# Masks of listed blocks moved into the rows of the feature tables (four graph-attention layers, one core)

## The chip, the cores and the metric

The kernel runs on one core of one Trainium2 chip. The metric is the device time of one execution in microseconds (us). TensorE (PE) multiplies matrices; its weight loads are shown as PEld. VectorE (DVE), ScalarE (ACT) and GpSimd (POOL) work on elements, SyncE (SP) issues DMAs. Indirect DMAs, which gather rows by a list of indices, are issued by GpSimd.

## The reference

Four layers of graph attention act on 4,096 nodes with 256 features, all with the same 4096 x 4096 adjacency. Each layer normalizes its input, applies a ReLU, and adds the attention's output to its input:

```
h = relu(layernorm(x))
layer 0: x += softmax(mask(leaky(s_i + t_j))) @ (h @ W.T + b)
layer 1: x += elu(softmax(mask(leaky(s_i + t_j))) @ (h @ W))
layer 2: four heads of 64 columns, each with its own s, t and W; no elu
layer 3: two softmaxes, of e and of -e; the two averages of h, the second negated,
         side by side, times wtrans, then elu
s, t = projections of the transformed rows (s by target node, t by source node)
```

Adjacency is random with a falling density: node i and node j are connected with a probability proportional to 1/sqrt((1+i)(1+j)), so early nodes have many sources and late ones few.

## The kernel before, in words

**Tiles.** Nodes stand in 32 tiles of 128 (NT). Targets are grouped in 8 blocks of 4 tiles (IT). Sources are grouped in chunks of 4 tiles (CH). The first chunk of sources (DP tiles) is always used in full ("pre").

**Dense and listed targets.** For a dense block, every source tile is used: one step weighs 128 sources for 512 targets on VectorE and multiplies them on TensorE (four matmuls of 128x257). For a listed target tile T, the used sources are collected in a list with room for CAPS[T] x 128 of them (6 to 12 for T from 4 on), and each step gathers 128 feature rows with an indirect DMA, weighs them and multiplies them once. DENSE = (4, 2, 1, 1) says how many blocks are dense in each layer; the others are listed. So layers 0 to 3 have 105, 174, 218 and 218 feature gathers.

**Where the operands come from.** Each layer's projected rows, with two more columns for the weights, are written to a DRAM table (`table[l]`, `node_rows`, lines 706 and 708) and gathered from there into `s_gg` (line 1189; pools of 7 buffers in layer 0, `gat0`, and 9 later, `gat`). In layer 0 the adjacency is read once: `mask_chunk` turns a loaded chunk into bytes on VectorE (line 1277) and writes it to `mask_t[b]`, one DRAM table for each block (line 1279). Dense blocks of layer 0 use the chunk at once; those of layers 1 to 3 load it back (`s_ms`, line 1390, beside the features `s_gs`, line 1388). For listed tiles, `gather_masks` (line 895) gathers the 128-byte mask rows of the same sources, once for each (T, k), into `mlist`, which stays on chip for all layers: 218 gathers in all.

**Lists.** In layer 0, blocks 4 to 7 are read as "side" chunks between the dense steps (`sides`). When all chunks of a block have been seen, `list_sources` builds its four lists, piece by piece.

**Order.** `run` walks a plan of steps written out by hand. Each step is fetched (gathers and loads are issued), begun, weighed and multiplied at fixed distances, LEAD = (0, 2, 3, 6), so that a step is multiplied six plan steps after its fetch. After each step, some pieces of other work are done: `posts` (projections for the next layer, ends of tiles), `lists_q` (list building) and `gather_masks`, in numbers given by `rates`. In layer 0, listed steps start beside the dense ones at plan step LISTED0 and are taken one or two at a time; layer 1 has 16 dense steps alone, then puts two dense steps behind each of its 24 listed tiles (16 to 31, then 8 to 15). In layers 2 and 3, tiles 8 to 31 come first and tiles 4 to 7 last. GpSimd's queue holds its instructions in just the order in which they are written; those of the other engines are ordered by a scheduler. A listed tile first makes sure that all masks of that tile are gathered.

**The end of a kernel.** A flag says whether a list was too short; then a dense version would run instead. It doesn't run with these inputs.

Of the kernel before, what the change touches and what calls it, by code (L numbers as in the profile page):

```python
# [8 lines left out]
F32 = mybir.dt.float32  # L9
F16 = mybir.dt.float16  # L10
U8 = mybir.dt.uint8
# [6 lines left out]
P = 128  # L18
N = 4096
D = 256  # L20
# [432 lines left out]

DP = CH
# [5 lines left out]
LISTED0 = 40  # L460
# [7 lines left out]
GW = tuple(h * p for h, p in zip(LH, PART))  # L468
LEAD = (0, 2, 3, 6)
# [3 lines left out]
def list_layers(ctx: ExitStack, tc: tile.TileContext, a: dict, out: bass.AP, flag):  # L473
# [38 lines left out]
    mask_t = [dram.tile([N + 1, IB], U8, name=f"mask_t{b}", tag=f"mask_t{b}") for b in range(NIB)]  # L512
    table = [dram.tile([N + 1, GW[l]], F32, name=f"table{l}", tag=f"table{l}") for l in range(4)]

    def table_rows(t, jt):

        r0 = jt // CH * CH * P
        r0 += 1 if r0 >= HALF else 0
        return t[r0 : r0 + CH * P, :].rearrange("(p k) d -> p k d", k=CH)

# [5 lines left out]
    def weights(l, pool, prep, q):  # L526
# [11 lines left out]
        L.table = table[l]  # L538
# [123 lines left out]
    def node_rows(L, T0):  # L662
# [29 lines left out]
        for k, T in enumerate(tiles):  # L692
# [3 lines left out]
            hT = rows.tile([P, 2, P], F32, name=f"s_hT_{u}_{k}", tag="hT")  # L696
# [4 lines left out]
        for k, T in enumerate(tiles):  # L701
# [3 lines left out]
            if L.l == 0 and T % CH == CH - 1:  # L705
                nc.sync.dma_start(table_rows(L.table, T), L.g[:, T - CH + 1 : T + 1, :])
            elif L.l > 0:
                nc.sync.dma_start(table_rows(L.table, T)[:, T % CH, :], g)
# [89 lines left out]
    def list_sources(ib, seen, pool, consts):  # L798
# [82 lines left out]

    masks_of = [
        (T, k)
        for b0, b1 in ((DENSE[0], NIB), (DENSE[1], DENSE[0]), (1, DENSE[1]))
        for T in range(b0 * IT, b1 * IT)
        for k in range(CAPS[T])
    ]

    def gather_masks(n, tile=None):

        for T, k in list(masks_of):
            if not n or tile is None and T not in index:
                break
            if tile in (None, T):
                nc.gpsimd.indirect_dma_start(  # L895
                    out=mlist[:, OFFS[T] + k, :],
                    out_offset=None,
                    in_=mask_t[T // IT],
                    in_offset=bass.IndirectOffsetOnAxis(ap=index[T][:, k : k + 1], axis=0),
                    element_offset=T % IT * P,  # L900
                )
                masks_of.remove((T, k))
                n -= 1

# [42 lines left out]
    class Unit:  # L947
# [4 lines left out]
        def __init__(u, L, T0, nt, n, get, big=None, heads=None, like=None, cost=1.7, nact=0, rates=(2, 0, 0), per=1):  # L952
# [205 lines left out]
    def run(plan):  # L1158

        n = len(plan)  # L1160
        for p in range(n + LEAD[3]):
# [5 lines left out]
            if p >= LEAD[3]:  # L1167
# [4 lines left out]
                gather_masks(u.rates[2])  # L1172


    def listed_sources(L, T, pool):
        heads = list(range(L.H))

        def get(i):
# [3 lines left out]
            else:  # L1182
                ensure(lambda: all(L.ready))
                while T not in index:
                    pump(lists_q, 1, force=True)
                gather_masks(CAPS[T], T)
                k = i - DP
                g = pool.tile([P, GW[L.l]], F32, name=f"s_gg_{L.l}_{T}_{k}", tag="gg")
                nc.gpsimd.indirect_dma_start(  # L1189
                    out=g,  # L1190
                    out_offset=None,
                    in_=L.table,
                    in_offset=bass.IndirectOffsetOnAxis(ap=index[T][:, k : k + 1], axis=0),
                )
                m = mlist[:, OFFS[T] + k, :]
            return heads, [g[:, h * L.part : (h + 1) * L.part] for h in heads], m
# [3 lines left out]
    with ExitStack() as phase:  # L1200
# [6 lines left out]
        gat0 = phase.enter_context(tc.tile_pool(name="s_gather0", bufs=7))  # L1207
# [10 lines left out]
        def zero_rows():  # L1218
# [3 lines left out]
            for b in range(NIB):  # L1222
                nc.sync.dma_start(mask_t[b][HALF : HALF + 1, :], zero[:, 0 : IB // 4].bitcast(U8))
            for l in range(4):
                for k in range(0, GW[l], D + 2):
                    n = min(D + 2, GW[l] - k)
                    nc.sync.dma_start(table[l][HALF : HALF + 1, k : k + n], zero[:, 0:n])
# [11 lines left out]
        sides = [2 + 3 * k for k in range((NIB - DENSE[0]) * NCH)]  # L1239
# [26 lines left out]
        def mask_chunk(ib, c):  # L1266
# [11 lines left out]
            if c > 0:  # L1278
                nc.sync.dma_start(table_rows(mask_t[ib], c * CH), m)
# [218 lines left out]
```

## Time and profile before

| what | value |
|---|---|
| median of 3 runs | 1940.74 us (1924.12 to 1942.46) |
| profiled execution | 1774.04 us |
| its span | 1771.9 us, mean clock of TensorE 0.959 |
| feature gathers on GpSimd (L1189) | 715, 745.0 us busy, 1042 ns each |
| mask gathers on GpSimd (L895) | 218, 240.9 us busy, 1105 ns each |
| moved by DMA | 271.08 MB, mean 153 GB/s |

The profile shows one execution. Busy time is a union of an engine's instructions; a busy TensorE is not a TensorE at its peak, since its matmuls are pipelined. "Idle before" is time in which an engine had nothing to run, put down to what ended it. In a table of stretches, every row is a stretch of time with each engine's busy us and number of instructions in it.

### The profile page before, as it was taken

The numbers are of one execution on the slowest core, as the hardware profiler recorded it, in microseconds if no ns is written. First come the engines' busy times: TensorE is split into PE (matmuls) and PEld (weight loads), VectorE is DVE, ScalarE is ACT, GpSimd is POOL, SyncE is SP. The second block draws the span as 40 slices with busy tenths as digits, with TensorE's granted clock in tenths as the row PEclk, the third lists the DMA queues.
The fourth block names the chain that finished last, engine by engine and source line by source line (L and its number), as shares of the span: only waits on it lengthen the run. The fifth ranks groups of instructions, "written<-read, shape, count | busy, mean of one in ns | idle before, by whom it ended". The sixth has DMA issues, their size and how long they took to land.

```text
span 1771.9 us, 29224 instructions
## 1 busy us (share of the span) xinstructions
PE 1670.8 (94%) x9268; PEld 1386.0 (78%) x9268; DVE 1331.1 (75%) x3908; ACT 610.2 (34%) x1802; POOL 1068.4 (60%) x1043
## 2 busy tenths in 40 slices
PE   6989999989999899897989999999999999999997
PEld 4877777768878778675467887889998888888886
DVE  6778898878764676654869988998886577777765
ACT  5531011011030132111357767699984011111101
POOL 9665655736566777777775444455571655555563
PEclk9998798989989999998999999999999999999999
DMA  8889767935264444443233333233332666656554
GB/s 270 275 268 296 221 208 230 333 103 184 53 167 138 119 130 136 119 130 88 66 75 97 85 104 86 80 105 104 91 101 74 206 201 181 181 168 183 168 171 125
DMA packets 134530, 271.08 MB, mean 153 GB/s; under 512 B 23186, under 2 KB 52288, under 8 KB 134368
## 3 DMA queue, kind: packets, MB, share of 16 engines
q0 software_dynamic: 48272, 127.55, 27.3%
q1 hardware_dynamic: 85260, 141.04, 24.0%
q8 instruction: 77, 1.26, 0.3%
q14 instruction: 85, 0.70, 0.1%
q10 hardware_dynamic: 836, 0.53, 0.1%
HBM read 228.91 MB, written 40.12 MB: 152 GB/s over the span
## 4 chain that ended last, share of the span: by engine, by line
PE 72%; DVE 10%; DMA 9%; POOL 4%; issue 3%; ACT 2%; SPq 0%; DVEq 0%; ACTq 0%; POOLq 0%
PE s_acc L1035 43%; PE s_accm L1060 17%; PE s_pj L727 6%; DMA s_gg<-table,idx 5%; DVE s_p L999 3%; DMA s_raw<-in_adjT 3%; PE idx_ps L866 2%; POOL mlist L895 2%; PE s_sT L933 1%; PE s_tp L695 1%; DVE first L857 1%; DVE s_m L1277 1%; POOL s_gg L1189 1%; ACT s_p L985 1%; DVE s_p L1008 1%
## 5 line engine op out<-in xcount | busy, mean ns | idle before, releaser
L1189 POOL DMA_INDIRECT s_gg<-table,idx x715 | 745.0, 1042 | 581.8 <-PE s_acc L1035 239.1
L999 DVE SCALAR_TENSOR_TENSOR s_p<-s_grow,s_gg,mlist 128x128 f32<-128x128 f32 x1151 | 367.8, 346 | 195.3 <-DMA s_gg<-table,idx 124.6
L1035 PE MATMUL s_acc<-s_gg,s_p 128*128 128x257 f32 x1430 | 358.1, 391 | 28.0 <-DVE s_p L999 27.7
L1035 PEld LDWEIGHTS s_acc<-s_gg,s_p 128*128 128x128 f32 x1430 | 267.5, 193 | 84.0 <-DVE s_p L999 48.4
L1035 PE MATMUL s_acc<-g,s_p 128*128 128x257 f32 x1152 | 298.3, 404 | 5.0 <-DVE s_p L999 5.0
L895 POOL DMA_INDIRECT mlist<-mask_t,idx x218 | 240.9, 1105 | 76.0 <-issue 56.4
L1035 PEld LDWEIGHTS s_acc<-g,s_p 128*128 128x128 f32 x1152 | 226.4, 202 | 38.2 <-DVE s_p L999 6.7
L999 DVE SCALAR_TENSOR_TENSOR s_p<-s_grow,pre,mpre 128x128 f32<-128x128 f32 (+1 forms) x576 | 190.3, 369 | 39.7 <-PE s_acc L1035 31.2
L1035 PE MATMUL s_acc<-s_gs,s_p 128*128 128x257 f32 x896 | 217.1, 398 | 0.0
L1060 PE MATMUL s_accm<-s_p,s_gg 128*65 128x128 f32 x1744 | 207.2, 274 | 3.4 <-DVE s_p L1008 2.7
L1035 PEld LDWEIGHTS s_acc<-s_gs,s_p 128*128 128x128 f32 x896 | 178.0, 200 | 32.0 <-DVE s_p L999 4.9
L1060 PEld LDWEIGHTS s_accm<-s_p,s_gg 128*65 128x65 f32 x1744 | 193.9, 138 | 8.6 <-DVE s_p L1008 5.1
L985 ACT ACTIVATE s_p<-s_grow,s_minus,s_gg 128x128 f32<-128x128 f32 x436 | 186.7, 486 | 36.8 <-DMA s_gg<-table,idx 23.1
L999 DVE SCALAR_TENSOR_TENSOR s_p<-s_grow,s_gs,s_ms 128x512 f32<-128x512 f32 x224 | 162.4, 749 | 45.0 <-PE s_accm L1060 21.0
L1035 PE MATMUL s_acc<-pre,s_p 128*128 128x257 f32 x768 | 181.8, 381 | 0.3 <-ACT s_y L1146 0.2
L727 PE MATMUL s_pj<-s_w,s_hT 128*128 128x259 f32 (+3 forms) x640 | 165.4, 399 | 7.7 <-ACT s_hT L697 3.7
L939 ACT ACTIVATE s_grow<-s_sT 128x256 f32<-128x256 f32 (+2 forms) x136 | 46.8, 367 | 341.8 <-PE s_sT L933 332.8
L1035 PEld LDWEIGHTS s_acc<-pre,s_p 128*128 128x128 f32 x768 | 143.4, 191 | 21.8 <-ACT s_y L1146 0.6
L727 PEld LDWEIGHTS s_pj<-s_w,s_hT 128*128 128x128 f32 x640 | 121.8, 197 | 31.5 <-ACT s_hT L697 6.4
L1060 PE MATMUL s_accm<-s_p,pre 128*65 128x128 f32 (+1 forms) x928 | 120.3, 284 | 4.8 <-DVE s_p L1008 4.8
L1060 PEld LDWEIGHTS s_accm<-s_p,pre 128*65 128x65 f32 x928 | 103.9, 138 | 21.6 <-issue 14.6
L985 ACT ACTIVATE s_p<-s_grow,s_minus,pre 128x128 f32<-128x128 f32 x224 | 96.3, 487 | 19.1 <-issue 11.9
(123 smaller groups left out, 1658.1 us busy)
## 6 DMA issues: line engine op xcount, KB each, us to landing
s_raw<-in_adjT SPq DMA_DIRECT2D x128, 512.0 KB
s_gs<-table SPq DMA_DIRECT2D x28, 516.0 KB
mask_t<-s_m SPq DMA_DIRECT2D x56, 256.0 KB
s_gg<-table,idx POOLq DMA_INDIRECT x715, 3.5
s_ms<-mask_t SPq DMA_DIRECT2D x35, 256.0 KB
table<-s_g SPq DMA_DIRECT2D x28, 258.0 KB
table<-g SPq DMA_DIRECT2D x8, 516.0 KB
x<-in_x SPq DMA_DIRECT2D x8, 512.0 KB
```

Source lines behind the costliest of these rows:

```text
L695: nc.tensor.transpose(tp[:, c, :], zs[k][:, c * P : (c + 1) * P], ident)
L727: nc.tensor.matmul(ps, lhsT=hT[:, c, :], rhs=L.w[:, c, k * (D + 6) : k * (D + 6) + cols], start=(c == 0), stop=(c == 1),)
L857: nc.vector.tensor_tensor(first, place, lof[:, t, j : j + half].unsqueeze(1).to_broadcast([P, P, half]), op=ALU.is_equal,)
L866: nc.tensor.matmul(ps[:, 0:cap], lhsT=first[:, :, j % half], rhs=val[:, 0:cap, j * IT + t], start=(j == 0), stop=(j == JT - 1),)
L895: nc.gpsimd.indirect_dma_start(out=mlist[:, OFFS[T] + k, :], out_offset=None, in_=mask_t[T // IT], in_offset=bass.IndirectOffsetOnAxis(ap= ...
L933: nc.tensor.transpose(ps[:, h - h0, it, :], L.s[:, T0 + it, h : h + 1].to_broadcast([P, P]), ident)
L939: nc.scalar.activation(grow[:, h1:h2, :], ps[:, h1 - h0 : h2 - h0].rearrange("p h a b -> p h (a b)"), AF.Exp, scale=scale,)
L985: nc.scalar.activation(w[:, h, :], u.grow[:, h, :], AF.Relu, scale=g[h][:, n - 1 : n], bias=minus)
L999: nc.vector.scalar_tensor_tensor(p[:, k, :], u.grow[:, h, :], g[k][:, n - 1 : n], m, op0=ALU.min if L.l == 3 and h == 1 else ALU.max, op1= ...
L1035: nc.tensor.matmul(u.accs[it][h], lhsT=p[:, k, it * P : (it + 1) * P], rhs=g[k][:, 0:n], start=first, stop=last,)
L1060: nc.tensor.matmul(u.regions[h], lhsT=g[k][:, 0 : DH + 1], rhs=p[:, k, :],  start=first and (u.nt > 1 or h == 0), stop=last, skip_group_ch ...
L1189: nc.gpsimd.indirect_dma_start(out=g, out_offset=None, in_=L.table, in_offset=bass.IndirectOffsetOnAxis(ap=index[T][:, k : k + 1], axis=0),)
```

## The change

All masks of listed blocks are stored in rows of the feature tables, beside the features of the same source node. MASKS_IN says where: block 1 lies in table 2, ahead of the features; block 2 in table 1 ahead and block 3 behind; blocks 4 and 5 in table 0 ahead and behind; blocks 6 and 7 in a second copy of layer 0's table (table 4). A listed tile's gather in the layer that holds its mask (layer 0 for blocks 4 to 7, layer 1 for 2 and 3, layer 2 for 1) takes the features and, in the same row, the part of the mask block that reaches to tile T's 128 bytes (128 to 512 bytes more). The weighting reads the mask from the gathered row; ScalarE copies it to `mlist` for later layers. `gather_masks` is gone. The table of block 0's masks stays alone, for dense blocks.

With it go: chunk 0 of the masks is also stored; layer 0's features are written twice (at block 6's side chunks); layer 0's gather pool has 6 buffers instead of 7, `hT` has 3 instead of 2; listed steps start at step 48 instead of 40 and come two for each dense step; side chunks come a little earlier; writes and loads of tables address columns within wider rows.

```diff
-LISTED0 = 40
+LISTED0 = 48
...
+MW = IB // 4
+MASKS_IN = {1: (2, False), 2: (1, False), 3: (1, True), 4: (0, False), 5: (0, True), 6: (4, False), 7: (4, True)}
+LAYER = (0, 1, 2, 3, 0)
+FRONT = tuple(MW * ((l, False) in MASKS_IN.values()) for l in range(5))
+TW = tuple(FRONT[l] + GW[LAYER[l]] + MW * ((l, True) in MASKS_IN.values()) for l in range(5))
...
-    mask_t = [dram.tile([N + 1, IB], U8, name=f"mask_t{b}", tag=f"mask_t{b}") for b in range(NIB)]
-    table = [dram.tile([N + 1, GW[l]], F32, name=f"table{l}", tag=f"table{l}") for l in range(4)]
+    table = [dram.tile([N + 1, TW[l]], F32, name=f"table{l}", tag=f"table{l}") for l in range(5)]
+    mask_t = dram.tile([N + 1, IB], U8, name="mask_t")
...
+    def feature_rows(l, jt):
+        return table_rows(table[l], jt)[:, :, FRONT[l] : FRONT[l] + GW[LAYER[l]]]
+
+    def mask_rows(b, jt):
+        if b == 0:
+            return table_rows(mask_t, jt)
+        l, behind = MASKS_IN[b]
+        c0 = FRONT[l] + GW[LAYER[l]] if behind else 0
+        return table_rows(table[l], jt)[:, :, c0 : c0 + MW].bitcast(U8)
...
-            hT = rows.tile([P, 2, P], F32, name=f"s_hT_{u}_{k}", tag="hT")
+            hT = rows.tile([P, 2, P], F32, name=f"s_hT_{u}_{k}", tag="hT", bufs=3)
...
-                gather_masks(u.rates[2])
...
-                gather_masks(CAPS[T], T)
                 k = i - DP
-                g = pool.tile([P, GW[L.l]], F32, name=f"s_gg_{L.l}_{T}_{k}", tag="gg")
+                at, behind = MASKS_IN[T // IT]
+                own = LAYER[at] == L.l
+                at = at if own else L.l
+                more = 0 if not own else (T % IT + 1 if behind else IT - T % IT) * MW // IT
+                wide = pool.tile([P, GW[L.l] + more], F32, name=f"s_gg_{L.l}_{T}_{k}", tag="gg")
+                front = 0 if behind else more
                 nc.gpsimd.indirect_dma_start(
-                    out=g,
+                    out=wide,
                     out_offset=None,
-                    in_=L.table,
+                    in_=table[at],
                     in_offset=bass.IndirectOffsetOnAxis(ap=index[T][:, k : k + 1], axis=0),
-                )
+                    element_offset=FRONT[at] - front,
+                )
+                g = wide[:, front : front + GW[L.l]]
                 m = mlist[:, OFFS[T] + k, :]
+                if own:
+                    c0 = (GW[L.l] + more) * 4 - P if behind else 0
+                    kept, m = m, wide.bitcast(U8)[:, c0 : c0 + P]
+                    nc.scalar.copy(kept, m)
...
-        gat0 = phase.enter_context(tc.tile_pool(name="s_gather0", bufs=7))
+        gat0 = phase.enter_context(tc.tile_pool(name="s_gather0", bufs=6))
...
-        sides = [2 + 3 * k for k in range((NIB - DENSE[0]) * NCH)]
+        sides = [2 + 3 * k - k // 8 for k in range((NIB - DENSE[0]) * NCH)]
...
-            if c > 0:
-                nc.sync.dma_start(table_rows(mask_t[ib], c * CH), m)
+            if c > 0 or ib in MASKS_IN:
+                nc.sync.dma_start(mask_rows(ib, c * CH), m)
+            if ib == 6:
+                ensure(lambda: all(L0.ready[c * CH : (c + 1) * CH]))
+                nc.sync.dma_start(feature_rows(4, c * CH), L0.g[:, c * CH : (c + 1) * CH, :])
...
-                    n = 1 + step[1] % 2
+                    n = 2
                     plan += listed[:n]
...
-                    rates=(2, 0, 1),
```

## The prediction

> **What bounds the kernel now.** I read the page's engine shares first, then a table of stretches (chosen where layers change), then GpSimd's timeline inside the worst stretch, then who waits for whom there. Shares:
>
> ```profile
> PE 1670.8 (94%) x9268; PEld 1386.0 (78%) x9268; DVE 1331.1 (75%) x3908; ACT 610.2 (34%) x1802; POOL 1068.4 (60%) x1043
> ```
>
> TensorE looks like the limit everywhere, and GpSimd (POOL) looks idle two fifths of the time. The table of stretches says otherwise (columns: stretch, length, then busy us with count for PE, PEld, DVE, ACT, POOL; then clock, DMA share, GB/s). Layer 0 is 0 to 514, layer 1 is 514 to 846, layer 2 runs to 1356, layer 3 is the rest.
>
> ```profile
> 100.00:300.00 200.00, 185.81 (x1067) 153.74 (x1067) 167.66 (x389) 33.59 (x119) 114.26 (x99) 0.85 0.75 237
> 514.00:716.00 202.00, 191.59 (x868) 158.84 (x869) 127.90 (x397) 44.70 (x159) 148.04 (x149) 0.97 0.50 139
> 716.00:846.00 130.00, 110.28 (x426) 81.39 (x425) 67.83 (x201) 21.14 (x69) 99.23 (x102) 0.88 0.42 111
> 846.00:894.00 48.00, 43.22 (x150) 20.99 (x149) 34.61 (x86) 14.59 (x50) 37.94 (x34) 0.96 0.25 61
> 1356.00:1772.00 416.00, 405.50 (x1898) 352.23 (x1896) 285.18 (x885) 52.65 (x138) 217.75 (x218) 0.99 0.59 172
> ```
>
> The reader sees that layer 3 keeps TensorE full at clock 0.99, while layer 1 loses time and clock, with GpSimd at 74% of it. GpSimd's own timeline there shows that 74% is all there is to have:
>
> ```profile
> 641.35 0.95 POOL L1189 DMA_INDIRECT s_gg<-table,idx  x1 [0.30 <-PE s_acc L1035]
> 642.60 0.95 POOL L1189 DMA_INDIRECT s_gg<-table,idx  x1 [0.30 <-PE s_acc L1035]
> 643.85 0.96 POOL L1189 DMA_INDIRECT s_gg<-table,idx  x1 [0.30 <-PE s_acc L1035]
> 645.12 1.02 POOL L895 DMA_INDIRECT mlist<-mask_t,idx  x1 [0.30 <-issue]
> 646.45 0.95 POOL L1189 DMA_INDIRECT s_gg<-table,idx  x1 [0.30 <-PE s_tp L695]
> 647.70 1.39 POOL L895 DMA_INDIRECT mlist<-mask_t,idx  x1 [0.30 <-DMA s_gg<-table,idx]
> ```
>
> One gather starts each 1.25 us, always 0.30 us after the one before, whatever releaser is named: the queue is full. Over layer 1 there are 250 gathers in 332 us, 1.33 us each; outside the 0.30 us gaps it idles only about 10 us. Those waiting are on the other side:
>
> ```profile
> DVE s_p L999 <- DMA s_gg<-table,idx: 82.7, 67, 4.7
> PEld s_acc L1035 <- DVE s_p L999: 51.9, 63, 2.4
> PE s_acc L1035 <- DVE s_p L999: 27.1, 35, 2.0
> ```
>
> VectorE waits for gathered rows, and TensorE for VectorE. So layer 1 is bound by the number of gathers, and layers 2 and 3 by TensorE. Layer 0 is mixed: DMA share 0.75 to 0.86, VectorE 84% busy, and GpSimd with pauses of 10 to 15 us before buffers come free.
>
> **What the Trainium skill says.** "Perfetto Trace Analysis", section "DMA Instruction — SWDGE (GPSIMD)", says that the recorded end of a gather is the end of writing its descriptors, not of the data. The trace agrees: 947 ns median on GpSimd, 3.5 us from issue to landing. Its section "What "DMA-bound" means" counts a solid issuing track as a limit of its own, which is what the timeline above shows. "TensorE: Matmul & The Clock Gate", Part 1, says that TensorE's clock follows how busy it has been, so a stall costs again as a slower clock; here the clock is 0.88 at 716 to 846 and 0.99 in layer 3. "ScalarE: Activation LUTs", section "What ACT_TABLE_LOAD costs", gives 186 ns + 0.833 ns an element for an instruction with immediates; the 128x256 copies (s_hT) took 372 ns here against 399, so I estimate a 128x128 copy at 0.28 us.
>
> **The change part by part.** The sum is made against the profiled execution: 1774.0 us, of which 1771.9 is the span. The median of the three runs is 1940.7, 167 us more.
>
> Removed: 218 mask gathers, 240.9 us of GpSimd plus 0.30 us each. The built order of GpSimd's queue holds 715 gathers after the change, none of masks alone. What counts is where they go:
>
> - Layer 1 has 76 of them (77.8 us busy) beside 174 feature gathers (169.4 us). Without them the queue needs 174 x (0.974 + 0.30) = 222 us. TensorE's work in the stretch: its records by shape count 1051 matmuls of 257 columns, 112 of 259 or 268, 104 of 128 and 26 small ones. In 1400 to 1700, where TensorE never stops, 1406 records took 300 us, 0.213 each. So 1051 x 0.213 + 112 x 0.222 + 104 x 0.13 + 26 x 0.1 = 265 us. The stretch lasts 332, so at most 67 us can go, and TensorE, not the gathers, is next in line. Not all goes: from 716 on, 70 gathers x 1.25 = 88 us meet about 426 x 0.21 = 89 us of matmuls. That is level, with nine buffers between them. I leave 12 us there and 8 for the copies below. Gain 47.
> - After layer 1, 32 more masks (block 1) fill the queue from 846 to 889, ahead of layer 2's first feature gather at 889. TensorE then stands for 4.8 us and limps for the first tiles (the line below). Gain 8.
> - Layer 0 has 108. GpSimd had pauses there, so their removal is covered by other work except near the end, where it issues back to back from 422 to 474 and from 494 on. Gain 4 together with the next point.
>
> ```profile
> 892.90 1.12 PE L1060 MATMUL s_accm<-s_p,pre 128*65 128x128 f32 x4 [4.78 <-DVE s_p L1008]
> ```
>
> Moved: layer 0's listed steps start at plan step 48 instead of 40, two per dense step instead of 1.5. That places 160 of 169 before the dense part ends instead of 132, so 9 instead of 37 trail behind. The side chunks of adjacency come up to three steps earlier, which asks 3% more of the loads.
>
> Added in layer 0: a second feature table (8 writes of 516 KB, 4.1 MB), seven mask chunks that were not stored (1.8 MB) and wider gathered rows (128 to 512 B more in place of a mask gather of 128 B: 105 x 128 x 192 B = 2.6 MB). 8.5 MB at the 284 GB/s of the first 100 us is 30 us of transfer. The mask rows are now 512 B pieces, 63 x 512 of them, instead of 56 x 128 pieces of 2 KB at 84 ns (38 us over 16 engines). Before shows no 512 B write; it lies between a quarter of 84 (42 us in all, +4) and the 46 ns of a 1 KB packet (93 us, +55). The DMA engines stand idle about a quarter of layer 0 until 430 us, some 110 us, which hides most. New waits: the first listed gather of each layer 0 table waits for every write of that table, behind the side chunk of step 46 (or 92) by two to four dense steps. Nothing but gathers is queued behind it; the weighting waits for them. Each second-table write stands on SP's queue behind its mask chunk's write, with the raw loads behind it. Buffers go from 7 to 6. Together I take 12 us; ends -5 and +45 (below nothing, because loads come a little earlier and the mask gathers' own transfers are gone).
>
> Added on ScalarE: 218 copies of 0.28 us, 61 us, each waiting for its gather to land, with everything behind it on ScalarE's queue (s_hT for projections, the elu's exponentials). In layers 0 and 1 ScalarE is 12 to 22% busy while they run; this is the 8 us above (0 to 25). In layer 2 the 44 copies of tiles 4 to 7 (12 us) meet ScalarE at 46.2 to 47.5 busy of each 50 us between 1200 and 1300. I take 5; 0 to 12.
>
> Free: the dense loads of layer 1 in 1 KB pieces (28 loads, several steps ahead) and the changed source of the mask operand (same 128x128 form). If their cover went, the loads would cost about 1 us each.
>
> Sum: -47 - 8 - 4 + 12 + 5 = -42, so 1732 of 1774.0. The median run is 9.4% longer and nothing shows where. If it is all a slower TensorE, layer 1 needs 265 x 1.094 = 290 us and at most 42 of 67 us are left to win; the sum falls to about -25. If everything is stretched alike, it is -46. I take -35: **1906**.
>
> **The rivals.**
> - TensorE is close behind. In the timed runs its work fills layer 1 almost alone, so only the trailing steps and layer 2's start gain: -12, 1929. For it: the 167 us, which fit a slower TensorE in layers 2 and 3. Against: VectorE's 82.7 us of waits are long, up to 4.7 us. Chance 0.22.
> - Slower: layer 0's transfers. If the 512 B pieces cost 46 ns, 55 + 30 = 85 us of DMA time come into the 110 idle, and SP's queue, which already waits between its loads, passes the delay to VectorE's masks and so to TensorE. From about 50 us of delay it outweighs the gain; at the worst some 60 of the 85 show, +25, 1966. Against: the raw loads wait for buffers (VectorE) rather than for transfers. Chance 0.15.
> - The whole 67 us of layer 1 are won and the copies cost nothing: -70, 1871. For it: layer 3 shows no stall at one gather in 1.9 us. Against: 716 to 846 stays level. Chance 0.13.
> - That the gathers don't vanish is excluded by the built order.
>
> **How the numbers follow.** The forecast has 0.50; its own range, from the unknown ends, is 1885 to 1925. Reaching to both neighbours for 8 in 10: 1868 to 1950. A measurement of this kernel tells about 1% from no change (19 us). Faster: nearly all of the forecast, the big gain and a little of the first rival, 0.63; within 1%: 0.22; slower: 0.15.
>
> **What would show it.** Right: layer 1's stretch falls from 332 us to about 285, with GpSimd waiting for buffers, and VectorE's wait for s_gg below 40 us; the clock there over 0.95; layer 2's first gather right after layer 1's end. Layer 0 ends near 520. Wrong: layer 0 beyond 540 with a DMA share over 0.9; layer 1 with ScalarE's copies waiting for gathers ahead of s_hT; or layer 1 still at one gather each 1.25 us.

## The result, and the profile after

| | median us | runs | ratio to before |
|---|---|---|---|
| before | 1932.43 (1921.49 to 1942.46) | 4 | |
| after | 1833.89 (1828.72 to 1839.67) | 4 | 0.9492 [0.942, 0.9564] |

The change gains 98 us, where I had forecast 35. Its profiled execution has a span of 1833.8 us.

One thing has to be known before the lines are read. Chips differ for this kernel: on two of the five used in the experiments the kernel before took 1929 and 1934 us (medians of 39 and 7 runs), on three 1766, 1764 and 1768 (31, 50 and 7 runs). The profile shown ahead of the prediction (1774 us) is of the second kind, the timed runs of the first. I call them the 1930 kind and the 1766 kind. Each chip was met in one batch alone, so a chip and its hour are not told apart. The profile after is of the 1930 kind, so that beside the profile of before it mixes two kinds; where that matters, runs of the same kind (e1 for before, g1 for after, both below) are named.

Shares of the whole, then the table of stretches (columns as in the prediction: busy us with count for PE, PEld, DVE, ACT, POOL; clock, DMA share, GB/s). Layer 0 now ends at 572, layer 1 at 889, layer 2 at 1408.

```profile
PE 1673.7 (91%) x9268; PEld 1397.5 (76%) x9268; DVE 1324.0 (72%) x3908; ACT 659.6 (36%) x2020; POOL 837.6 (46%) x825
```

```profile
100.00:300.00 200.00, 168.22 (x937) 136.78 (x937) 151.66 (x354) 40.02 (x144) 48.56 (x42) 0.88 0.85 250
572.00:773.00 201.00, 189.71 (x882) 161.29 (x881) 126.33 (x391) 46.06 (x165) 113.08 (x112) 0.97 0.49 137
773.00:889.00 116.00, 96.31 (x410) 79.88 (x409) 63.45 (x191) 36.39 (x134) 60.64 (x63) 0.90 0.47 132
889.00:937.00 48.00, 46.50 (x189) 24.49 (x188) 40.06 (x106) 20.33 (x65) 11.34 (x12) 1.00 0.26 75
1408.00:1834.00 426.00, 411.12 (x1913) 356.13 (x1911) 282.41 (x889) 53.16 (x139) 227.32 (x218) 0.99 0.57 168
```

GpSimd is no longer full in layer 1 (113 of 201 us in place of 148 of 202), and layer 2 starts with TensorE busy 46.5 of 48 us at full clock. But from 100 to 300, in layer 0, TensorE got through 937 matmuls, where the kernel before on the same kind of chip (e1) got through 1003; on the 1766 kind it is 936 (g1) in place of 1067. The line of e1:

```profile
100.00:300.00 200.00, 175.17 (x1003) 144.11 (x1003) 162.24 (x380) 31.38 (x110) 106.12 (x95) 0.87 0.73 232
```

GpSimd's timeline in layer 1 shows groups of gathers with pauses for buffers:

```profile
726.96 0.95 POOL L1187 DMA_INDIRECT s_gg<-table,idx  x1 [0.30 <-issue]
730.65 1.05 POOL L1187 DMA_INDIRECT s_gg<-table,idx  x1 [2.75 <-PE s_acc L1029]
732.01 1.41 POOL L1187 DMA_INDIRECT s_gg<-table,idx  x1 [0.30 <-PE s_acc L1029]
```

The waits in layer 1 (engine and line, what ended the wait: us in total, times, longest):

```profile
ACT mlist L1199 <- DMA s_gg<-table,idx: 62.0, 46, 4.4
DVE s_p L993 <- DMA s_gg<-table,idx: 12.5, 9, 4.1
```

VectorE's wait for gathered rows is 12.5 us here and 10.1 in g1, against 82.7 in the profile before. On the 1930 kind there was no such wait to remove: e1 has 6.3. ScalarE now waits for the same rows, at the head of its queue. In layer 0 it does so more, and two waits of loads stand beside it:

```profile
ACT mlist L1199 <- DMA s_gg<-table,idx: 247.0, 96, 21.9
POOL s_gg L1187 <- DMA s_raw<-in_adjT: 71.7, 1, 71.7
DVE s_m L1279 <- DMA s_raw<-in_adjT: 50.7, 32, 4.4
```

The length of each layer (from its first matmul to that of the next, worked out from TensorE's timeline), one execution of each kernel that the argument needs:

| kernel, kind of chip | layer 0 | layer 1 | layer 2 | layer 3 | span |
|---|---|---|---|---|---|
| before, 1766 (the profile shown) | 520 | 326 | 506 | 419 | 1772 |
| after, 1766 (g1) | 573 | 296 | 493 | 419 | 1781 |
| no mask gathers, 1766 (g2) | 503 | 273 | 494 | 419 | 1688 |
| before, 1930 (e1) | 555 | 419 | 526 | 432 | 1932 |
| after, 1930 | 572 | 316 | 519 | 426 | 1834 |
| no mask gathers, 1930 (e2) | 515 | 300 | 520 | 428 | 1762 |

On the 1930 kind the gain is layer 1's (103 us) and layer 0 gives 17 back. On the 1766 kind layers 1 and 2 win 43 and layer 0 loses 53. A single execution can lie apart from its median: g1's profile (1782.9 us) is the slowest of 20 with a median of 1771.9, g2's (1689.8) the fastest of 4 with a median of 1697.4.

### The profile page after: what moved, and what is told of

Same layout as the page of the kernel before. It is cut to its first block, busy times and chain, and to the rows that moved or that the text cites. A ratio compares the mean times of both kernels' runs of the same rounds, so it can differ in the third digit from the quotient of the medians.

```text
span 1833.8 us, 29170 instructions
## 1 busy us (share of the span) xinstructions
PE 1673.7 (91%) x9268; PEld 1397.5 (76%) x9268; DVE 1324.0 (72%) x3908; ACT 659.6 (36%) x2020; POOL 837.6 (46%) x825
## 4 chain that ended last, share of the span: by engine, by line
PE 60%; issue 3%; ACT 3%; DVE 2%; DMA 2%; another core or an unknown queue 1%; POOL 0%; POOLq 0%; ACTq 0%; DVEq 0%
PE s_acc L1029 32%; PE s_accm L1054 20%; PE s_pj L745 5%; DMA s_gg<-table,idx 2%; PE s_sT L927 1%; ACT s_p L979 1%; DVE s_p L993 1%; PE s_tp L713 1%; PE s_oT L1116 0%; POOL s_gg L1187 0%; PE idx_ps L884 0%; DVE s_p L1002 0%; ACT mlist L1199 0%; ACT s_e L1092 0%
## 5 line engine op out<-in xcount | busy, mean ns | idle before, releaser
L1187 POOL DMA_INDIRECT s_gg<-table,idx x715 | 755.3, 1056 | 948.8 <-PE s_acc L1029 292.5
L1029 PE MATMUL s_acc<-s_gg,s_p 128*128 128x257 f32 x1430 | 350.6, 391 | 11.9 <-DVE s_p L993 9.9
L993 DVE SCALAR_TENSOR_TENSOR s_p<-s_grow,s_gg,mlist 128x128 f32<-128x128 f32 x889 | 275.3, 348 | 118.0 <-PE s_acc L1029 61.9
L1029 PEld LDWEIGHTS s_acc<-s_gg,s_p 128*128 128x128 f32 x1430 | 275.0, 196 | 56.4 <-DVE s_p L993 13.0
L1029 PE MATMUL s_acc<-s_gs,s_p 128*128 128x257 f32 x896 | 204.0, 381 | 0.0
L1029 PEld LDWEIGHTS s_acc<-s_gs,s_p 128*128 128x128 f32 x896 | 169.6, 190 | 24.5 <-DVE s_p L993 0.8
L745 PE MATMUL s_pj<-s_w,s_hT 128*128 128x259 f32 (+3 forms) x640 | 172.0, 413 | 14.6 <-ACT s_g L780 8.1
L1199 ACT COPY mlist<-s_gg 128x128 uint8<-128x128 uint8 x218 | 63.9, 296 | 325.2 <-DMA s_gg<-table,idx 313.0
L745 PEld LDWEIGHTS s_pj<-s_w,s_hT 128*128 128x128 f32 x640 | 126.8, 206 | 41.8 <-ACT s_g L780 10.0
L1279 DVE TENSOR_SCALAR s_m<-s_raw 128x1024 uint8<-128x1024 int32 x112 | 80.6, 728 | 53.0 <-DMA s_raw<-in_adjT 50.7
```

The source lines that it names most:

```text
L745: nc.tensor.matmul(ps, lhsT=hT[:, c, :], rhs=L.w[:, c, k * (D + 6) : k * (D + 6) + cols], start=(c == 0), stop=(c == 1),)
L993: nc.vector.scalar_tensor_tensor(p[:, k, :], u.grow[:, h, :], g[k][:, n - 1 : n], m, op0=ALU.min if L.l == 3 and h == 1 else ALU.max, op1= ...
L1029: nc.tensor.matmul(u.accs[it][h], lhsT=p[:, k, it * P : (it + 1) * P], rhs=g[k][:, 0:n], start=first, stop=last,)
L1187: nc.gpsimd.indirect_dma_start(out=wide, out_offset=None, in_=table[at], in_offset=bass.IndirectOffsetOnAxis(ap=index[T][:, k : k + 1], ax ...
L1199: nc.scalar.copy(kept, m)
L1279: nc.vector.tensor_scalar(m[:, h * half : (h + 1) * half, :], raw, 0.0, None, op0=ALU.is_gt)
```

## Experiments

Each batch ran on one chip beside the kernel before. My theory after the result was that the forecast had the place right (gathers in layer 1) and the base wrong. The rivals were that order, copies or layout did it, or that TensorE had been slow everywhere.

### First batch: a chip of the 1930 kind

**e1, the kernel before once more.** No edit.

> The kernel before, unchanged, profiled a second time, because its first profile (1774 us) lies 160 us below its own timed runs, while the changed kernel's profile (1836 us) agrees with its timed runs. Theory G (the gain lies in GpSimd's queue of gathers): a profile near 1930 us shows layer 1 near 430 us with a gather every 1.6 us or more, since the 100 us that the change wins must have been lost there. Rival P (TensorE slower in the timed runs): the clock in layers 2 and 3 is under 0.9 and their 926 us grow to over 1000. Timed against itself: 1.00.

Measured: 1932.5 us, ratio 0.9995 [0.9967, 1.0022], span 1932.3. This execution agrees with the timed runs. (That 1774 was no chance either is shown by the second, third and fifth batch.) In the table, e1 is longer than the profile shown by 35 us in layer 0, 93 in layer 1, 20 in layer 2 and 13 in layer 3. A TensorE slower everywhere is refuted: layer 3, which TensorE fills, is 3% longer, layer 1 28%. Its layer 1, as one stretch:

```profile
555.00:974.00 419.00, 302.05 (x1281) 246.03 (x1280) 193.59 (x579) 64.91 (x225) 261.51 (x267) 0.86 0.36 97
```

GpSimd's share is down to 62% (82% with the 0.30 us before each of the 267), so the queue of gathers alone is not what holds layer 1 here. The waits in 555 to 1000 name a new releaser, "remote", which is the profile's word for a semaphore event that it finds no instruction for:

```profile
ACT s_grow L939 <- remote: 89.5, 9, 48.7
DVE s_p L999 <- remote: 82.1, 25, 12.0
```

In the whole execution there are 63 such waits over 0.4 us, 261 us together, some 205 of them in layer 1. By the semaphore that the trace gives for each wait, all of them wait for TensorE. The profile shown before the prediction has none. The timeline of the longest (all engines, start first):

```profile
911.82 1.92 PE L933 MATMUL s_sT<-s_ident,s_s 128*128 128x128 f32 x8
913.53 1.06 PE L1035 MATMUL s_acc<-s_gg,s_p 128*128 128x257 f32 x2
...
932.89 0.35 DVE L999 SCALAR_TENSOR_TENSOR s_p<-s_grow,s_gg,mlist 128x128 f32<-128x128 f32 x1 [12.01 <-remote]
...
955.72 0.94 POOL L895 DMA_INDIRECT mlist<-mask_t,idx  x1 [0.30 <-issue]
961.60 0.60 ACT L939 ACTIVATE s_grow<-s_sT 128x512 f32<-128x512 f32 x1 [48.73 <-remote]
962.25 1.11 PE L933 MATMUL s_sT<-s_ident,s_s 128*128 128x128 f32 x4 [47.65 <-ACT s_grow L939]
```

ScalarE reads `s_sT`, which TensorE's record begins at 911.82; it gets it at 961.60. I read this as completions of TensorE that come late, while TensorE counts as idle and waits for ScalarE. (The end of a matmul's record is modelled, so the record doesn't exclude that TensorE itself was slow.) The granted clock was 0.50 from 918 to 969. The Trainium skill, "TensorE: Matmul & The Clock Gate", Part 1, "Seeing it yourself", warns that clock records have been unreliable and the gate has been seen stuck at a quarter for over 50 us. The length fits; the clock on record is a half, not a quarter, and no run shows that the clock is what holds the completions back.

Two more things lie in the traces. First, on the 1930 kind many updates of semaphores are missing from the records: in e1 TensorE's semaphore has 2339 for 2707 instructions that raise it, VectorE's 2593 for 3579, ScalarE's 1086 for 1414. All kernels of this kind show it, those without mask gathers too (e2: 2368 for TensorE). On the 1766 kind the counts agree within two. So who released a wait is less sure on the 1930 kind; the lengths of the layers don't depend on it. What is left on record is late for TensorE alone: 313 of its updates in e1 come more than 0.5 us after the nearest end of a matmul before them (184 in e2, 2 in the profile before), and 2 each for VectorE and ScalarE.

Second, of the 32 moments in e1 at which a "remote" wait of over 1.5 us ends, 23 lie in a pause of GpSimd of over 0.45 us, though such pauses fill only 30% of the time from 200 to 970, where most of them lie. In the changed kernel, without mask gathers, all five do. Either gathers issued back to back hold the completions up, or GpSimd pauses because late completions keep its buffers from coming free. No run tells which.

**e2, no mask gathers.** Both calls of `gather_masks` go.

```diff
-                gather_masks(u.rates[2])
...
-                gather_masks(CAPS[T], T)
...
-                m = mlist[:, OFFS[T] + k, :]
+                m = onesu
```

> The kernel before without its 218 mask gathers, everything else as it was (layout, start of listed steps, seven buffers): listed steps weigh with a tile of ones instead of the mask, so the masks are left out of listed tiles. Theory G: the whole gain or more, 1800 to 1840 us (ratio 0.93 to 0.95). Rival S (the gain is in the new order of listed steps): under 40 us are gained, over 1890.

Measured: 1763.45 us, 0.9112 [0.9042, 0.9182]. The gathers, with the waiting for them, are worth 169 us on this kind (from e1's 1932.5), more than the whole change gains; "remote" waits are down to 33 us (and to 34 in the changed kernel).

**e3, the order alone.**

```diff
-LISTED0 = 40
+LISTED0 = 48
...
-tag="hT")
+tag="hT", bufs=3)
...
-bufs=7))
+bufs=6))
...
-        sides = [2 + 3 * k for k in range((NIB - DENSE[0]) * NCH)]
+        sides = [2 + 3 * k - k // 8 for k in range((NIB - DENSE[0]) * NCH)]
...
-                    n = 1 + step[1] % 2
+                    n = 2
```

> The kernel before with the changed kernel's order alone: listed steps from plan step 48, two per dense step, side chunks earlier, six gather buffers in layer 0, three of hT; masks still gathered alone. Theory G: within 20 us of before. Rival S: 50 to 100 us faster.

Measured: 1935.8 us, 1.0045 [1.0021, 1.007]. The order brings none of the gain. Its "remote" waits stay (228 us), and its layer 0 is 12 us longer than e1's (567 against 555).

**e4, the changed kernel without copies.**

```diff
-                m = mlist[:, OFFS[T] + k, :]
+                m = onesu
                 if own:
                     c0 = (GW[L.l] + more) * 4 - P if behind else 0
-                    kept, m = m, wide.bitcast(U8)[:, c0 : c0 + P]
-                    nc.scalar.copy(kept, m)
+                    m = wide.bitcast(U8)[:, c0 : c0 + P]
```

> The changed kernel without ScalarE's 218 copies; layers that don't gather a mask with the features weigh with a tile of ones, so their listed masks are left out. If the copies and the waits behind them on ScalarE cost what was forecast (13 us): 1820. If they cost nothing: 1834. If ScalarE's queue behind them is what makes layer 0 of the changed kernel long (570 us): 1780 or less.

Measured: 1788.17 us, 0.9265 [0.9186, 0.9344]: 46 us under the changed kernel. So of 169 us the changed kernel gives back about 70: 46 through the copies, 25 otherwise.

### Second batch: a chip of the 1766 kind

These were made to find out what in a mask gather disturbs TensorE, and met a chip on which nothing disturbs it. None of the four has a "remote" wait. They tell instead what a mask gather costs there.

**f1, 44 gathers fewer.**

```diff
-        for b0, b1 in ((DENSE[0], NIB), (DENSE[1], DENSE[0]), (1, DENSE[1]))
+        for b0, b1 in ((DENSE[0], NIB), (DENSE[1], DENSE[0]))
```

> The kernel before, with the masks of block 1 (44 of the 218) not gathered; tiles 4 to 7 weigh with ones instead, so that their masks are left out. Theory A: the 169 us that the mask gathers cost sit where TensorE falls silent, above all between 897 and 962 us in the second profile of the kernel before, which is just where the 44 gathers of block 1 run back to back: 50 to 65 us fewer, about 1875. Theory B: every mask gather costs alike, 169/218 = 0.78 us each: 34 us fewer, about 1898. Theory C, from my prediction: layer 2 starts 8 us sooner and nothing more: 1924.

Measured: 1751.0 us, 0.989 [0.9838, 0.9941], so -15. Layer 2 (492 us for 506) has nearly all of it: this is the term that I had put at -8.

**f2 and f3, another size and another target.** f3 is the same with 128 B and the old offset.

```diff
-    mlist = keep.tile([P, NLIST, P], U8, name="mlist")
+    spare = [keep.tile([P, 512], U8, name=f"spare{j}") for j in range(8)]
...
-                    out=mlist[:, OFFS[T] + k, :],
+                    out=spare[(OFFS[T] + k) % 8],
...
-                    element_offset=T % IT * P,
+                    element_offset=0,
...
-                m = mlist[:, OFFS[T] + k, :]
+                m = onesu
```

> The kernel before, with each of the 218 mask gathers fetching the whole 512 B row of its block instead of 128 B, into eight spare tiles in turn; listed steps weigh with ones, so that the masks are left out and nobody waits for these gathers. Beside it the same with 128 B. If the number of gathers on GpSimd's queue is what costs, both stay near 1930. If it is their small pieces that disturb other engines, this one comes down towards 1763 (the kernel with no mask gathers), to under 1850, and the other stays.

> As the one with 512 B, but 128 B from each row as before, into eight spare tiles in turn; listed steps weigh with ones, so that the masks are left out. It tells whether the waiting of steps for their masks is the cost: then it is near 1763 although all 218 gathers are issued. If it is the gathers themselves, it stays at 1920 to 1940.

Measured: 1770.9 us, 1.0019 [1.0002, 1.0037], and 1766.7 us, 1.0005 [0.9984, 1.0027]. Neither four times the bytes nor the waiting of steps for masks matters.

**f4, a memset for each gather.**

```diff
-                nc.gpsimd.indirect_dma_start(
-                    out=mlist[:, OFFS[T] + k, :],
...
+                nc.gpsimd.memset(spare, 0.0)
```

> The kernel before, with each of the 218 mask gathers replaced by a GpSimd memset of 128x1400 f32 (I expect 1.1 to 1.3 us each, as long as a gather with its gap) at the same place in the queue; listed steps weigh with ones, so that the masks are left out. If the time that GpSimd's queue loses to masks is the cost, about 1930. If it is something that the DMAs of a gather do, near 1763.

Measured: 1790.05 us, 1.0124 [1.0078, 1.0171]. A group of its profile shows how long the stand-in was:

```profile
L897 POOL MEMSET spare<- 128x1400 f32 x218 | 287.7, 1320 | 5.9
```

1.32 us without a gap, against 1.105 + 0.30 for a gather. The total alone would mislead, for the stand-in has a cost of its own: VectorE's 297 TENSOR_SCALAR instructions took 723 ns on the mean beside 482 in f3, and layer 0 lasts 551 us in place of 514. The reading rests on layer 1: 317 us with memsets, 327 with gathers that nobody waits for (f3), 273 without either (g2, on another chip of this kind). So instructions that issue no DMA cost there most of what the gathers cost. On this kind the cost of a mask gather in layer 1 is mainly its place in GpSimd's queue. That fits what the Trainium skill says of a solid issuing track, that it is a limit of its own ("Perfetto Trace Analysis", section "What "DMA-bound" means").

### Third batch: another chip of the 1766 kind

**g1, the changed kernel again.** No edit.

> The changed kernel once more, unchanged. The kernel before took 1930 us on the chip of the first four experiments, with 261 us of waits for TensorE completions that came later than TensorE's own records say, and 1766 us on the chip of the next four, with none. If the gain of 98 us is the removal of those late completions, then where the kernel before takes about 1930 this one takes about 1834 again, and where the kernel before takes about 1766 the gain shrinks to what my sum gave for such an execution (-42, about 1724) or, if copies and layout cost the 70 us measured on the first chip, turns into a loss of about 10 (1775).

Measured: 1771.9 us beside 1764.3, ratio 1.0049 [1.0033, 1.0065]. Where no completion is late the change gains nothing; the sum of the prediction, made for this kind, was -42.

**g2, no mask gathers, as e2.**

> The kernel before without its 218 mask gathers (listed steps weigh with ones; the masks are left out), as in the first batch. Where the kernel before takes 1930: 1763 again. Where it takes 1766: my reading of layer 1 (gathers bound it, 67 us to TensorE's own work, and 8 and 4 elsewhere) says -60 to -79, about 1695; if TensorE is close behind, -25, about 1740.

Measured: 1697.4 us, 0.9644 [0.9601, 0.9686], so -67. That this equals the 67 us of layer 1 in the prediction is chance: by stages layer 1 gives 53, layer 2 12 and layer 0 17, in two executions 84 us apart. But the reading of layer 1 was right for the kind of chip that the profile came from. One line each for layer 1 of before, of after and without gathers:

```profile
520.00:846.00 326.00, 298.27 (x1279) 237.83 (x1278) 191.04 (x578) 64.10 (x223) 242.80 (x245) 0.93 0.46 126
```

```profile
573.00:869.00 296.00, 277.10 (x1289) 236.17 (x1288) 189.94 (x578) 82.63 (x298) 172.28 (x174) 0.97 0.50 145
```

```profile
503.00:775.00 272.00, 268.50 (x1279) 229.67 (x1278) 188.20 (x574) 64.39 (x223) 172.12 (x174) 1.00 0.51 145
```

Without gathers TensorE is busy 268.5 of 272 us at full clock, close to the floor of 265 that I had counted. The changed kernel stays 23 us above it.

In layer 0 the same three kernels part ways the other way round. First after, then before, from 300 to 500:

```profile
300.00:500.00 200.00, 171.26 (x901) 138.56 (x902) 139.01 (x350) 35.23 (x129) 57.17 (x49) 0.81 0.60 184
```

```profile
300.00:500.00 200.00, 188.35 (x1086) 158.98 (x1086) 163.05 (x432) 26.17 (x96) 123.50 (x109) 0.93 0.53 167
```

VectorE and TensorE both do less. What VectorE waits for in 200 to 500, after and before:

```profile
DVE s_m L1279 <- DMA s_raw<-in_adjT: 29.9, 16, 4.4
```

```profile
DVE s_m L1277 <- DMA s_raw<-in_adjT: 6.8, 7, 2.6
```

The adjacency loads come later, and TensorE's clock is 0.81 in place of 0.93. On the 1930 kind the same wait is there without copies (28.2 us in h4).

**f5, copies on VectorE, and f6, copies at multiply time.**

```diff
-                    nc.scalar.copy(kept, m)
+                    nc.vector.tensor_copy(kept, m)
```

```diff
-                    nc.scalar.copy(kept, m)
+                    held_back[L.l, T, i] = kept, m
...
             heads, g, p = u.steps.pop(i)
+            if (L.l, u.T0, i) in held_back:
+                nc.scalar.copy(*held_back.pop((L.l, u.T0, i)))
```

> The changed kernel with the 218 mask copies on VectorE in place of ScalarE. If it is ScalarE's queue standing behind the copies that costs the 46 us of the first batch, most of it comes back: 30 to 45 us under the changed kernel. If VectorE, with 72% of the span busy, takes the load no better (218 x 0.2 us, each waiting for a landing ahead of the weighing), it stays within 15 us of it or gets slower.

> The changed kernel with each mask copy issued on ScalarE when its step is multiplied, six plan steps after its gather, in place of at once. If the 46 us are waiting for gathers to land at the head of ScalarE's queue (147 waits, 313 us in the changed kernel's trace), nearly all of it comes back: about 40 us under the changed kernel. If they are the copies' own 64 us of ScalarE, nothing changes.

Measured: 1769.6 us, 1.0028 [1.0014, 1.0042], and 1771.7 us, 1.0038 [1.0021, 1.0056]; the changed kernel had 1.0049. Neither won the 30 to 45 us that waiting at the head of ScalarE's queue would have given back: where the copies stand makes no difference to the time on this kind. That ScalarE's queue behind them costs the 46 us of e4 is not shown.

### Fourth batch: a chip of the 1930 kind

h2, h3 and h4 are rungs from the kernel without mask gathers (1763.5, e2) to the changed one (1833.9). h1 asks whether half of the change is better than all.

**h1, layers 1 and 2 alone.**

```diff
-MASKS_IN = {1: (2, False), 2: (1, False), 3: (1, True), 4: (0, False), 5: (0, True), 6: (4, False), 7: (4, True)}
+MASKS_IN = {1: (2, False), 2: (1, False), 3: (1, True)}
...
+    masks_of = [
+        (T, k)
+        for b0, b1 in ((DENSE[0], NIB),)
+        for T in range(b0 * IT, b1 * IT)
+        for k in range(CAPS[T])
+    ]
...
+                gather_masks(u.rates[2])
```

Layer 0's order, buffers and single table are those of before, and its 105 listed steps have their masks gathered alone.

> Half of the change: masks of blocks 1, 2 and 3 lie beside the features of layers 1 and 2, as in the changed kernel; those of blocks 4 to 7 are gathered alone in layer 0, as before, and layer 0 has one table, seven buffers and the order of before. If layer 0's part of the change is what gives the gain back (by the stages, 53 us longer on the third chip while layers 1 and 2 win 43), this beats both kernels: about 1720 where the kernel before takes 1765, about 1800 where it takes 1930. If the loss lies in the copies, or in layer 1 as well, it stays near 1765 (or 1834).

Measured: 1814.25 us, 0.9376 [0.9338, 0.9414]: 20 us under the changed kernel. "Remote" waits are 29 us, though a mask is gathered alone 105 times in layer 0: on this kind most of the late completions come with the mask gathers of layer 1.

**h2 (e2 with e3's edit), h3 (e4 with one table) and h4 (e4 again).** h3's edit to e4:

```diff
-                own = LAYER[at] == L.l
+                own = LAYER[at] == L.l and at < 4
...
-            if ib == 6:
-                ensure(lambda: all(L0.ready[c * CH : (c + 1) * CH]))
-                nc.sync.dma_start(feature_rows(4, c * CH), L0.g[:, c * CH : (c + 1) * CH, :])
```

> The kernel without mask gathers (ones for masks), with nothing of the change but the order of layer 0: listed steps from 48, two for each dense step, earlier side chunks, six buffers, three hT. First rung between the kernel without gathers (1697 on the third chip) and the changed kernel (1772). If order and buffers cost nothing, 1697 (1763 on the first chip); if the loss is there, 1730 or more.

> The changed kernel without copies and without the second table of layer 0: masks are stored in rows as 512 B pieces, blocks 4 and 5 gather theirs beside the features of layer 0, blocks 6 and 7 gather features alone from the first table; where no mask was gathered, steps weigh with ones. Second rung: to h2 it adds the pieces in rows (masks and layer 0's features). If those cost, by 30 to 50 us over h2; if not, within 10 of it, and the second table or the copies carry the loss.

> The changed kernel without the copies on ScalarE, as in the first batch (layers that don't gather their masks weigh with ones). Third rung: to h3 it adds the second table and its wider gathers. On the first chip it was 46 us under the changed kernel. Moving the copies made no difference on the third chip, so here I expect 10 to 25 us under the changed kernel (1750 to 1760), unless the copies' waiting costs only on the first chip: then 1770.

Measured: 1780.1, 1785.9 and 1798.0 us; ratios 0.9189 [0.9148, 0.9231], 0.9222 [0.918, 0.9263], 0.9297 [0.9258, 0.9336]. The rungs are then: order and buffers 17 us, pieces in rows 6, second table 12, copies 36 (46 in e4). Only the last stands clear: the intervals of the ratios overlap from each rung to the next before it. The 17 also compares two chips, between which the same kernel (e4, h4) differs by 10. By stages the rungs lie in layer 0: 515, 528, 540, 545 and, with copies, 572 us (one execution each; e4 has 540). The copies also lengthen layer 1 from 300 to 316. The order costs layer 0 about as much beside gathers (12 us in e3) as without them (13).

### Fifth batch: a chip of the 1766 kind

**i1 (h1 again) and i2 (f4 again).**

> The kernel that keeps the change in layers 1 and 2 alone, unchanged. It took 1814 where the kernel before took 1934. There, 1814 again. On a chip where the kernel before takes about 1765: the stages of the changed kernel there (layer 1 296 us in place of 326, layer 2 493 in place of 506) with layer 0 as before give -43, about 1722; if layer 0 still loses through masks of blocks 1 to 3 in 512 B pieces, about 1740.

> The kernel before with each mask gather replaced by a GpSimd memset as long as one (1.32 us), weighed with ones, as in the second batch, where it took 1790 beside 1766 for the kernel before. On a chip where the kernel before takes about 1930: if TensorE's late completions come from GpSimd's queue being full in layer 1, they stay, and it takes 1920 to 1960. If they come from what the gathers move or write, it takes about 1790 to 1820. On the other kind of chip: 1790 again.

Measured: i1 1725.5 us, 0.9761 [0.974, 0.9782], as summed from the stages (1722). i2 1794.7 us, 1.0145 [1.0117, 1.0172], as before. Layer 0 of i1 lasts 516 us and layer 1 295, so half of the change beats both kernels on both kinds of chip: 1725 against 1768 and 1772, 1814 against 1934 and 1834. It also stores the masks of blocks 1 to 3 in 512 B pieces, and layer 0 is as long as in f2 and f3 (514), so these pieces show no cost there. i2, whose layers are those of f4 (556 and 317), was meant for the other kind and leaves its question open.

## Why the prediction failed

**The step that failed first is "The median run is 9.4% longer and nothing shows where".** I offered two readings, a slower TensorE or everything stretched alike, and took -35 between them. Both were wrong. The difference sits for 93 of 160 us in layer 1, where the change acts, with waits that I read as late completions of TensorE and that fall from 261 to 33 us when the mask gathers are left out. On the 1930 kind the gathers are worth 169 us in place of 67, and the change won 98. That the kernel got faster as forecast is luck as far as the sum goes: for its own kind of chip it said -42, and g1 measured +8. By its own terms the first reading (42 us left to win in layer 1) gives -17 and not -25.

**Layer 1 (-47).** Measured -30 on the kind of chip of the profile, -103 on the other. The gathers as the bound and TensorE's floor were right for the profile's kind: without them 326 us became 273, 8 above the floor of 265, where I had left 12. (The 67 were counted from 514, six us before layer 1's first matmul.) The 8 us for copies became 23 for all that the change adds there (296 against 273). What of it the copies are was measured on the 1930 kind alone: 16.

**Layer 2's start (-8) and its copies (+5).** The stall of 4.78 us is gone and layer 2 is 13 us shorter in the changed kernel and in the one without gathers alike. So the start was worth 12 to 14, and the 44 copies added less than a us to layer 2 beside ScalarE's full load.

**Layer 0 (-4 and +12).** This term was mis-sized most on the profile's own kind: +53. Leaving the gathers out gives -17, so what is added costs 70 in these executions. By the medians g1 and g2 lie 74 us apart, of which layer 1 has 23, so I estimate some 50 (f5 and f6, by their medians as fast as g1, have a layer 0 of 554 and 562); both are above my upper end of 45. The rival on the slow side, layer 0's transfers, showed its signs: layer 0 reaches 573 us with the DMA engines 0.91 busy in the first 200 (0.84 in the profile before), VectorE waits for raw loads, and the changed kernel is slower than before by 0.5% on that kind. Its cause is not shown: how the 70 divide on the 1766 kind was not measured, and on the 1930 kind the copies are the only part that stands clear, while the two rungs of transfers come to 6 and 12. I had priced the added bytes against idle DMA time and the copies against layers 1 and 2 alone; for the copies in layer 0 I had put nothing beside the 8 us of layer 1, and on the 1930 kind they are 27 to 32 us there (572 against 545 and 540). The price of a 512 B piece, which I had left between 21 and 46 ns, is 27 ns at the median of the 32256 in g1's trace: 54 us for the 63 x 512 of them in place of 38, so +16 and not the +55 of that rival.

**Signs.** GpSimd waiting for buffers and a wait for `s_gg` below 40 us came as written; a clock over 0.95 in layer 1 came on the profile's kind (0.97 in g1) and not in the second half of layer 1 on the other (0.90). Layer 1 at about 285 and layer 0 near 520 did not come. Of the signs of being wrong two came: layer 0 beyond 540 with a DMA share over 0.9 (in its first 200 us), and ScalarE's copies waiting for gathers in layer 1 (60 us in g1).

**Against the rivals.** TensorE close behind (-12) was refuted by g2: 53 us of layer 1 can be had. That all 67 are won came true on the profile's kind in neither kernel (53 without gathers, 30 with the change); on the other kind layer 1 won more than was on the table, for a reason that none of the rivals held. The slow side is told under layer 0.

**What stays open.** Why TensorE seems to complete late on two of five chips, why mask gathers in layer 1 bring it on, and whether the recording of the profile, which misses semaphore updates on just these chips, takes part. A full queue of GpSimd, the gathers' transfers and the steps' waiting for masks were to be told apart by f2 to f4, but all three ran where nothing is late. Nor is it shown why layer 2 without mask gathers takes 520 us on the one kind and 494 on the other. So the larger part of the measured gain is located, not explained.

## What to carry to other kernels

If the profiled execution and the timed runs differ by several per cent, as here, the difference need not be a factor to scale a sum by: profile the kernel again until one execution matches the timed runs, and see in which stage they part. Taking gathers out of a full queue paid in the stages that the queue bounded. In layer 0, which it did not bound, what replaced them cost more than they did (573 against 520 us), so such a layout is best applied stage by stage, as i1 shows. And a stand-in has to be priced by stages too: f4's memsets filled GpSimd's queue as wanted, and slowed VectorE elsewhere.

## What the runs showed of the hardware

- On two of five chips updates of TensorE's semaphore stand up to 47 us after the nearest recorded end of a matmul before them (e1). The waits then carry the name "remote", most of them on VectorE and ScalarE (261 us in e1, none in the profile shown), and TensorE looks idle. The kernel before differs by 9% between these chips and the others; without mask gathers it is still 1763 against 1697, 4%.
- A memset of 128x1400 f32 on GpSimd takes 1.32 us, and beside 218 of them VectorE's TENSOR_SCALAR instructions took 723 ns on the mean (f4) in place of 482 (f3); its SCALAR_TENSOR_TENSOR instructions stayed at 403.
- A gather of 128 rows takes GpSimd about as long for 128 B as for 512 B a row:

```profile
L897 POOL DMA_INDIRECT spare<-mask_t,idx x218 | 238.7, 1095 | 78.1 <-issue 58.8 <-DVE idx L878 11.4 <-DMA spare<-mask_t,idx 3.9
```

  That is f2 (512 B), 1095 ns each; f3 (128 B) has 1109. Rows of 1 to 2 KB (`s_gg`) have 1036 to 1037 in the same two kernels.
- A DMA packet of 512 B took 27 ns at the median (32256 of them in g1), one of 1 KB 46 and one of 2 KB 84.
